# Reordering the start of a two-layer attention and experts kernel, with gate weights, PSUM pools and two operations moved between engines

## The chip, the core and the metric

The kernel runs on one core of a Trainium2 chip. The metric is device time in microseconds (us) of one execution. The core has TensorE (PE, with its weight loads shown apart as PEld), VectorE (DVE), ScalarE (ACT), GpSimd (POOL) and SyncE (SP), which here issues DMAs. Each engine runs its own instructions in order and waits for others on semaphores.

## The reference

The input x is 8 batches of 512 tokens of 256 values, in float32. There are two layers, each a layer norm, two branches, and a residual sum:

```python
xn = _layernorm(x)
x = x + attention(xn) + experts(xn)      # first layer
xn = _layernorm(x)
x = x + reads(xn) + blocks(xn)           # second layer
```

The attention has 16 heads of 64. Queries and keys are RMS-normalised by head. Scores get a bias of distance times a slope by head (`softplus(omega)` times a fixed slope) times a gate by query token, which is `softplus` of the raw-normalised key times a unit vector u by head, over 8:

```python
q = _rmsnorm(q, q_rms_w); k = _rmsnorm(k, k_rms_w)
u_n = u / jnp.maximum(jnp.linalg.norm(u, axis=-1, keepdims=True), U_L2_EPS)
gate = jax.nn.softplus(jnp.einsum('bthd,hd->bht', k, u_n) / math.sqrt(D))
bias = -dist * omega_eff * gate          # causal, then softmax over the scores
```

The experts branch takes 32 experts; each picks 8 tokens of each batch by a softmax over the tokens, merges them, runs a GELU network of 1024 hidden values, and gives the result back to the picked tokens. The second layer is a small GELU read and a block network of 16 blocks, of which each token uses 4.

## The kernel before

**Tiling.** Tokens of a batch are 4 tiles of 128. Heads are in 4 groups of 4, so that there are 32 pieces of work (8 batches by 4 groups), numbered n. `produce(n)` (L584) makes queries, keys, values and gate logits of a group: for each of 4 tiles, `pq` (queries and keys, one 128x512 PSUM tile, L597), `pv` (values and gate logits, L605), a square on ACT (L612), a sum by head on DVE (L629), mean (L632), an inverse root on POOL (L205), the scaled copy `tm` on DVE (L639), its transposes `pqk` (L655), and the copies qT on ACT and kT on DVE (L660, L667). `gate` (L693) then makes the gate's series on DVE (L305 to L312), splits it into bfloat16 parts on POOL (L730 to L751), and turns it (L768, L775: gT). `attend(u)` (L789) does one of 8 units of a group: scores (L807 with the bias rows `bst` and gT, L811 with qT and kT), the maximum (L820), exp (L828), reciprocal (L835), the division on POOL (L838), the transposes `pp` (L851), copies (L859, L861), and after four units the values `y` (L885). `output` (L903) projects (L915).

**Before the first group.** `norm_rows` (L383) loads a batch, takes statistics (L408, L410, L412), an inverse root on POOL (L414), normalises on DVE (L417), transposes (L425) and copies (L434, L436). The first batch goes tile by tile, the other seven whole. `gate_weights` (L340) folds u into the key weights: for a group, squares and sums of u (L347, L351), the root on POOL (L358), floor and reciprocal (L354, L361), u times that and times the key norm's weights (L362, L364), then two products with the key weights and two sums (L368, L370). Their results are the last 4 columns of `wvg_sb`, which `pv` reads. POOL makes the constants of the scores: `masks` (L236) and `bias_rows` (L244 to L261), and the zeros of `mT` (L264). `choose(half)` (L482) picks tokens for the experts once 4 batches are normalised (`lg` L493, `pst` L516, `pmg` L528, `pmT` L541); `expert` (L974) follows.

**What sets the order.** Every piece is an `op` of a class `Plan` (L49): an engine, a cost in ns, a function that issues the instructions, what it depends on, a priority in attention units, and slots that it takes and gives back (`acq`, `rel`: PSUM and SBUF buffers). `emit` (L67) walks a model of the five engines. At each step it takes the operation that can start first, the one of lowest priority where two are equal, of those within 12 units (`AHEAD`) of the lowest priority still open, and issues it. So the costs and priorities fix the order in which each engine's queue is written; at run time only semaphores and those queues count. Three PSUM pools have two buffers each: `mm`, `sc`, `tr` (L173 to L175). SP is the only issuer of DMAs (`load`, L266, whose cost is 60 unless given; weights have 655).

The priorities that matter: u at -19, weights of the first group at -18, gate weights at -17 for the first group and at -1, 1, 3 for the others, `masks` and `bias_rows` at -8 and -7 with no dependency, batches 1 to 3 at 2, 4, 6, the first choice at 8, batches 4 to 7 at 10 to 16, the second choice at 18.5, experts from unit 32 on in steps of 6.5.

Of the kernel before, what the change touches and what calls it, by code (L numbers as in the profile page):

```python
# [15 lines left out]
P = 128  # L16
# [123 lines left out]
def tile_two_layer_block(  # L140
# [82 lines left out]
    with tc.tile_pool(name="pb", bufs=2) as pb, tc.tile_pool(name="pb1", bufs=1) as pb1:  # L223
# [20 lines left out]
        def bias_rows():  # L244
            nc.gpsimd.iota(bst, pattern=[[0, NPR], [1, T]], base=-MID, channel_multiplier=0,
                           allow_small_or_imprecise_dtypes=True)

            for h in range(2):
                k = slice(h * D, (h + 1) * D)
                for q in range(NPR):  # L250
                    r0 = 2 * NSP * q
                    for first, fill in ((r0 + NSP, 1.0), (r0 + 2 * NSP, 0.0)):
                        nc.gpsimd.affine_select(
                            out=bst[k, q, :], in_=bst[k, q, :], compare_op=ALU.is_ge, fill=fill,
                            base=first - 1, pattern=[[0, T]], channel_multiplier=-1,
                        )
                    if q:
                        nc.gpsimd.affine_select(
                            out=bst[k, q, :], in_=bst[k, q, :], compare_op=ALU.is_ge, fill=0.0,
                            base=-r0, pattern=[[0, T]], channel_multiplier=1,  # L260
                        )  # L261

        consts = [op("POOL", 2000, masks, (), -8.0), op("POOL", 5500, bias_rows, (), -7.0)]
        zeros = op("POOL", 2000, lambda: nc.gpsimd.memset(mT, 0.0), (), 4.0)  # L264

        def load(dst, src, prio, cost=60, acq=()):  # L266
            return op("DMA", cost, lambda: nc.sync.dma_start(dst, src), (), prio, acq=acq, lat=2000)
# [3 lines left out]
        for g in range(NHG):  # L271
            at = -18.0 if g == 0 else -9.0 + g
            w_qk[g], w_v[g] = [], []
            heads = slice(g * GW, (g + 1) * GW)
            for dc in range(NC):
                rows = slice(dc * P, (dc + 1) * P)
                w_qk[g].append(load(wqk_sb[:, dc, g, GW:], wk[rows, heads], at, 655))
            for dc in range(NC):
                rows = slice(dc * P, (dc + 1) * P)
                w_qk[g].append(load(wqk_sb[:, dc, g, :GW], wq[rows, heads], at + 0.1, 655))  # L280
                w_v[g].append(load(wvg_sb[:, dc, g, :GW], wv[rows, heads], at + 0.2, 655))
# [4 lines left out]
            load(w128[h * D : (h + 1) * D, k : k + 1], r.unsqueeze(1), -15.5)  # L286
# [34 lines left out]
        for k, f in enumerate(log1p_steps(lambda: oz, lambda: oy, lambda: oy2, lambda: om_sb)):  # L321
# [12 lines left out]
        v_u = [  # L334
            load(ub, u.rearrange("h d -> (h d)").partition_broadcast(P), -19.0, 600, acq=["eh"]),
            load(kwb, k_rms_w.partition_broadcast(P), -18.9, acq=["gT"]),
        ]
        w_g = {}

        def gate_weights(g, at):  # L340
            m = Grp()
            mine = ub3[:, g * HG : (g + 1) * HG, :]
            wide = lambda k: wqk_sb[:, k, g, GW:].rearrange("p (h d) -> p h d", d=D)

            def squares():
                m.sq = pb.tile([P, 2 * HG, D], F32, tag="sq", name=f"usq_{g}", bufs=1)
                nc.vector.tensor_mul(m.sq[:, :HG], mine, mine)  # L347

            def norms():
                m.un = pb.tile([P, HG], F32, tag="un", name=f"un_{g}")  # L350
                nc.vector.tensor_reduce(m.un, m.sq[:, :HG], AX.X, ALU.add)  # L351

            def floor():
                nc.vector.tensor_scalar(m.un, m.un, U_EPS, None, ALU.max)  # L354

            d = [op("DVE", 334, squares, v_u, at, acq=["sq"])]
            d = [op("DVE", 334, norms, d, at + 0.01)]
# [18 lines left out]
        for g in range(NHG):  # L376
            gate_weights(g, -17.0 if g == 0 else -3.0 + 2 * g)
# [1233 lines left out]
```

## Time and profile before

| what | us |
|---|---|
| median of 3 runs | 1491.2 (1490.54 to 1491.31) |
| the profiled execution's own time | 1489.48 |
| its span, first to last instruction | 1487.8 |
| PE busy | 1430.8 |
| DVE, ACT, POOL busy | 906.4, 715.0, 600.4 |
| first transpose of tokens on PE (L425) | 16.39 after the span's start |
| first scores (L807) | 63.45 |

The span is the time from the first to the last instruction of one execution; about 1.7 us lie outside it. A row of the timeline has the start, the length, the engine, the line of the program, the operation, what it writes and reads, the count of merged instructions, and in brackets how long the engine was idle before it and what it waited for. A row of busy time by windows has, after the stretch and its length, the busy us and the count of instructions for PE, PEld, DVE, ACT and POOL, then the granted clock of PE (1.00 is full), the busy share of the DMA engines, and GB/s.

### The profile page before, as it was taken

Reading aid. Unit: us, or ns where it says so; the run is one execution under the profiler, and the core shown is the slowest. Engines: PE = TensorE matmul, PEld = TensorE weight load, DVE = VectorE, ACT = ScalarE, POOL = GpSimd, SP = SyncE. Lnnn points to the kernel's source line nnn. Section 1 sums busy time; section 2 is a strip of 40 time slices with the busy share of each in tenths; the row PEclk is TensorE's granted clock in tenths of the full one; section 3 lists DMA queues with packets and bytes.
Section 4 is the critical chain, followed back from the end, with each engine's and each line's share of the span. In section 5 each row is a group of like instructions: output and inputs, shape, how many; then the busy total and the mean of one; then the engine's idle time right before and its main releaser. Section 6 shows DMA issues by size and latency. Waiting matters only on the chain.

```text
span 1487.8 us, 25107 instructions
## 1 busy us (share of the span) xinstructions
PE 1430.8 (96%) x8317; PEld 866.3 (58%) x8332; DVE 906.4 (61%) x3461; ACT 715.0 (48%) x1928; POOL 600.4 (40%) x1109
## 2 busy tenths in 40 slices
PE   3999999999999999999999999999999899999999
PEld 1555556556655665566556655665566466566666
DVE  6888776676677667766776677667766632322210
ACT  1455555555555556555655565655554531222221
POOL 5544554454454345444454454445444421111100
PEclk9999999999999999999999999999999999999999
DMA  6010111232231321232132213122220000000000
GB/s 203 4 57 1 61 61 60 73 111 65 81 102 59 103 85 57 63 105 80 58 118 65 65 62 114 65 69 85 79 74 9 1 15 15 11 18 15 19 15 22
DMA packets 74688, 90.19 MB, mean 61 GB/s; under 512 B 5800, under 2 KB 57760, under 8 KB 74560
## 3 DMA queue, kind: packets, MB, share of 16 engines
q1 hardware_dynamic: 74560, 88.59, 18.4%
q8 instruction: 67, 1.10, 0.3%
q14 instruction: 61, 0.50, 0.1%
HBM read 84.11 MB, written 4.19 MB: 59 GB/s over the span
## 4 chain that ended last, share of the span: by engine, by line
PE 86%; DVE 8%; ACT 3%; issue 1%; POOL 1%; DMA 1%; SPq 0%; ACTq 0%; DVEq 0%; POOLq 0%
PE pq L597 14%; PE pp L851 9%; PE y L885 8%; PE sc L811 8%; PE ph L1497 8%; PE py L1544 7%; PE po L915 7%; PE pv L605 7%; PE pqk L655 4%; PE sc L807 4%; PE peo L1052 2%; PE ph L992 2%; DVE pr L820 1%; ACT pr L828 1%; DVE ss L629 1%
## 5 line engine op out<-in xcount | busy, mean ns | idle before, releaser
L838 POOL TENSOR_SCALAR pr<-pr,rinv 128x384 f32<-128x384 f32 (+3 forms) x512 | 266.2, 533 | 324.9 <-DVE rinv L835 243.2
L828 ACT ACTIVATE pr<-pr,nm 128x384 f32<-128x384 f32 (+3 forms) x512 | 284.2, 557 | 112.6 <-DVE nm L820 72.8
L205 POOL TENSOR_TENSOR rsqk<-ss,nhalf 128x8 f32<-128x8 f32 x128 | 210.6, 1646 | 218.2 <-DVE ss L632 199.0
L820 DVE CUSTOM_DVE_ANT_0 pr<-sc,later 128x384 f32<-128x384 f32 (+3 forms) x512 | 238.8, 483 | 39.1 <-PE sc L811 35.7
L597 PE MATMUL pq<-wqk_sb,xnT 128*128 128x512 f32 x512 | 248.4, 608 | 2.6 <-DVE gl L623 2.6
L851 PE MATMUL pp<-ident,pr 128*128 128x128 f32 x1280 | 220.0, 282 | 10.6 <-POOL pr L838 2.8
L851 PEld LDWEIGHTS pp<-ident,pr 128*128 128x128 f32 x1280 | 149.7, 141 | 128.6 <-issue 67.8
L811 PE MATMUL sc<-kT,qT 64*128 64x384 f32 (+3 forms) x1024 | 181.9, 437 | 0.0
L859 ACT COPY prT<-pp 128x384 f32<-128x384 f32 (+3 forms) x256 | 107.6, 423 | 147.3 <-PE pp L851 146.4
L861 DVE COPY prT<-pp 128x384 f32<-128x384 f32 (+3 forms) x256 | 124.2, 486 | 72.1 <-PE pp L851 68.4
L885 PE MATMUL y<-prT,v 128*64 128x512 f32 (+3 forms) x1024 | 152.9, 439 | 2.2 <-ACT prT L859 1.8
L605 PE MATMUL pv<-wvg_sb,xnT 128*128 128x260 f32 x512 | 138.3, 393 | 2.3 <-DVE tm L639 2.3
L597 PEld LDWEIGHTS pq<-wqk_sb,xnT 128*128 128x128 f32 x512 | 88.5, 193 | 78.2 <-issue 67.1
L612 ACT ACTIVATE sq<-pq 128x512 f32<-128x512 f32 x128 | 76.2, 595 | 113.9 <-PE pq L597 98.9
L885 PEld LDWEIGHTS y<-prT,v 128*64 128x64 f32 x1024 | 69.1, 136 | 96.4 <-issue 65.3
L1497 PE MATMUL ph<-xT,mT 128*128 128x512 f32 x256 | 121.1, 595 | 0.6 <-DVE nm L820 0.2
L915 PE MATMUL po<-wp_sb,yT 128*128 128x256 f32 x512 | 116.1, 380 | 0.1
L629 DVE TENSOR_REDUCE ss<-sq 128x8 f32<-128x512 f32 x128 | 87.0, 680 | 37.8 <-ACT sq L612 37.5
L605 PEld LDWEIGHTS pv<-wvg_sb,xnT 128*128 128x128 f32 x512 | 89.6, 192 | 32.3 <-issue 9.4
L639 DVE TENSOR_TENSOR tm<-pq,rsqk 128x512 f32<-128x512 f32 x128 | 87.8, 686 | 31.7 <-POOL rsqk L205 30.8
L915 PEld LDWEIGHTS po<-wp_sb,yT 128*128 128x128 f32 x512 | 95.1, 190 | 13.0 <-issue 0.3
L1552 DVE TENSOR_TENSOR ot<-py,x 128x256 f32<-128x256 f32 x32 | 13.6, 424 | 143.7 <-PE py L1544 143.7
(259 smaller groups left out, 1885.4 us busy)
## 6 DMA issues: line engine op xcount, KB each, us to landing
ew<-in_L_ffn_w_dram SPq DMA_DIRECT2D x128, 512.0 KB
xr<-in_L_attn_x_dram SPq DMA_DIRECT2D x32, 128.0 KB
out_dram<-ot SPq DMA_DIRECT2D x32, 128.0 KB
x<-in_L_attn_x_dram SPq DMA_DIRECT2D x7, 512.0 KB
raw<-in_L_ffn_w_dram SPq DMA_DIRECT2D x4, 512.0 KB
wqk_sb<-in_L_attn_Wk_dram SPq DMA_DIRECT2D x8, 128.0 KB
wqk_sb<-in_L_attn_Wq_dram SPq DMA_DIRECT2D x8, 128.0 KB
wvg_sb<-in_L_attn_Wv_dram SPq DMA_DIRECT2D x8, 128.0 KB
```

What stands on the lines that cost most here:

```text
L205: nc.gpsimd.tensor_tensor(r, src, nhalf[:, :n], ALU.pow)
L597: nc.tensor.matmul(s.pq[t], xnT[b][:, dc, cols], wqk_sb[:, dc, g, :], start=(dc == 0), stop=(dc == NC - 1),)
L605: nc.tensor.matmul(s.pv[t][:, : GW + HG], xnT[b][:, dc, cols], wvg_sb[:, dc, g, :], start=(dc == 0), stop=(dc == NC - 1),)
L811: nc.tensor.matmul(m.sc[:, h, :w], s.qT[k, q, n0:w], s.kT[k, q, :w], start=False, stop=True)
L820: nc.vector.tensor_tensor_reduce(m.p[:, h, :], m.sc[:, h, :w], later[:, T - w :], -1.0, BIG, ALU.add, ALU.min, m.nm[:, h : h + 1],)
L828: nc.scalar.activation(m.p[:, h, :], m.p[:, h, :], AF.Exp, bias=m.nm[:, h : h + 1], scale=-1.0, accum_out=m.sums[:, h : h + 1],)
L838: nc.gpsimd.tensor_scalar(m.p[:, h, :], m.p[:, h, :], m.rinv[:, h : h + 1], 1.0, ALU.mult, ALU.mult)
L851: nc.tensor.transpose(m.pt[h][:, d * P : (d + 1) * P], m.p[:, h, j * P : (j + 1) * P], ident)
L861: nc.vector.tensor_copy(dst, src)
L885: nc.tensor.matmul(pp.yp[h * D : (h + 1) * D, j * P :], s.v[j][:, hh * D : (hh + 1) * D], pp.tri[:, h, j : j + 4 * (NT - 1 - j) + 1 : 4, : ...
L915: nc.tensor.matmul(o.po[:, :C], yT[b * nk + k][:, t * P : (t + 1) * P], wp_sb[:, k, :], start=(k == 0), stop=(k == nk - 1),)
L1497: nc.tensor.matmul(m.ph[:, i, :], w1T[:, dc, k * P : (k + 1) * P], s.xT[:, dc, :], start=(dc == 0), stop=False,)
```

## The change

It has these parts.

1. **Order.** `masks` and the new `row_scales` depend, in the plan, on the roots of the first gate weights and of the first batch (`first`). A new op `begun` issues nothing; it depends on the first group's queries, keys and gate rows, and the gate weights of the other groups, the statistics of batches 1 to 7 and the transposes of the experts' gate wait for it in the plan. Batches 1 to 3 go to 5, 10, 15, the first choice to 19, batches 4 to 7 to 21, 25, 29, 33, the second choice to 38, and the experts start 16 units later with steps of 6.0.
2. **Loads.** Weights of a group are one DMA each for keys, queries and values, not two; u is loaded by group (128 KB, not 512 KB at once). Those of the first group's u and values, and of the key norm's weights, are issued by ACT. Costs of loads in the plan are 470 to 900.
3. **Gate weights.** The square is on ACT. The key weights are multiplied with u times the norm's weights, for both halves at once, while the root is taken, and the sums are multiplied with the reciprocal at the end.
4. **Score rows.** `bst` is made of a ramp `pos` by two ACT instructions (scale and bias by partition), with small selects on POOL; before, an iota and ten selects on POOL of 512 columns.
5. **Norms.** For batches 1 to 7 the normalised tokens are written by ACT, with a small DVE step ahead (`nb`).
6. **PSUM.** In the first group, `pq` of tiles 0 and 1 is in `sc` and every `pv` in `tr`. In every group a `pq` follows, in the plan, the `pv` before the last.
7. The zeros of `mT` are eight memsets, not one.

```diff
-        consts = [op("POOL", 2000, masks, (), -8.0), op("POOL", 5500, bias_rows, (), -7.0)]
-        zeros = op("POOL", 2000, lambda: nc.gpsimd.memset(mT, 0.0), (), 4.0)
+        pos = pb.tile([P, T], F32, tag="pr1", name="pos", bufs=1)
+        rows = pb1.tile([P, 2, NPR], F32, tag="rows", name="rows")
+        def row_scales():
+            nc.gpsimd.iota(pos, pattern=[[1, T]], base=-MID, channel_multiplier=0,
+                           allow_small_or_imprecise_dtypes=True)
+            nc.gpsimd.memset(rows, 1.0)
+            for h in range(2):
+                k = slice(h * D, (h + 1) * D)
+                for j in range(2):
+                    first = NSP * j
+                    nc.gpsimd.affine_select(
+                        out=rows[k, j, :], in_=rows[k, j, :], compare_op=ALU.is_ge, fill=0.0,
+                        base=-first, pattern=[[-2 * NSP, NPR]], channel_multiplier=1,
+                    )
...
+        def bias_rows(q):
+            nc.scalar.activation(
+                bst[:, q, :], pos, AF.Identity, bias=rows[:, 1, q : q + 1],
+                scale=rows[:, 0, q : q + 1],
+            )
...
+            w_qk[g] = [
+                load(wqk_sb[:, :, g, GW:], both(wk), at, 900),
+                load(wqk_sb[:, :, g, :GW], both(wq), at + 0.1, 900),
+            ]
+            w_v[g] = [load(wvg_sb[:, :, g, :GW], both(wv), at + 0.2, 900, by=by)]
...
+        begun = op("POOL", 1, lambda: None, (), -6.9)
...
+            d = [op("ACT", 272, squares, v_u[g] + ([begun] if g else []), at, acq=["sq"])]
+            s = [op("DVE", 334, lambda: nc.vector.tensor_reduce(
+                m.un, m.sq[:, :HG], AX.X, ALU.add), d, at + 0.01)]
             d = [op("DVE", 334, lambda: nc.vector.tensor_mul(
-                mine, mine, m.un.unsqueeze(2).to_broadcast([P, HG, D])), d, at + 0.05)]
+                mine, mine, kwb.unsqueeze(1).to_broadcast([P, HG, D])), d, at + 0.015)]
+            r = [op("POOL", 1030, lambda: nc.gpsimd.tensor_tensor(m.un, m.un, phalf, ALU.pow),
+                    s, at + 0.02)]
...
+            d = [op("DVE", 598, products, d + s + w_qk[g][:1], at + 0.07)]
+            d = [op("DVE", 598, lambda: nc.vector.tensor_reduce(
+                m.gw.rearrange("p k h -> p (k h)"), m.sq, AX.X, ALU.add), d, at + 0.08)]
+            w_g[g] = [op("DVE", 86, lambda: nc.vector.tensor_mul(
+                wvg_sb[:, :, g, GW:], m.gw, m.un.unsqueeze(1).to_broadcast([P, NC, HG])),
+                d + r, at + 0.09, rel=["sq"] + (["eh", "gT"] if g == NHG - 1 else []))]
...
-            gate_weights(g, -17.0 if g == 0 else -3.0 + 2 * g)
+            gate_weights(g, -15.95 if g == 0 else -3.0 + 2 * g)
...
+                    if b:
+                        xn = op("ACT", 370, lambda t=t: nc.scalar.activation(
+                            m.x[:, t, :], m.x[:, t, :], AF.Identity, bias=m.ve[:, t : t + 1],
+                            scale=m.rs[:, t : t + 1]), [nb], a_ + 0.1)
...
+        first = roots[:1] + roots[-NT:]
+        consts = [op("POOL", 1000, masks, first, -8.0)]
+        sc_ = op("POOL", 2000, row_scales, first, -7.9, acq=["pr1"])
+        for q in range(NPR):
+            consts.append(op("ACT", 485, lambda q=q: bias_rows(q), [sc_], -7.0,
+                             rel=["pr1"] if q == NPR - 1 else []))
         for b in range(1, BPG):
-            norm_rows(b, 2.0 * b, [list(range(NT))])
-        choose(0, 8.0)
+            norm_rows(b, 5.0 * b, [list(range(NT))])
+        choose(0, 19.0)
         for b in range(BPG, B):
-            norm_rows(b, 10.0 + 2.0 * (b - BPG), [list(range(NT))])
-        choose(1, 18.5)
+            norm_rows(b, 21.0 + 4.0 * (b - BPG), [list(range(NT))])
+        choose(1, 38.0)
...
+                qk_in = "sc" if n == 0 and t < 2 else "mm"
+                v_in = "mm" if n else "tr"
...
-                a = op("PE", 1716, q_k, x_T[b] + w_qk[g], at + w, acq=["mm"])
+                a = op("PE", 1716, q_k, x_T[b] + w_qk[g] + vals[-2:-1], at + w,
+                       acq=[qk_in])
...
         for n in range(NIT):
             produce(n)
+            if n == 0:
+                begun.deps += grp[0].ready
...
-        step = (NIT - NHG - 2) * NU / (4 * NG)
+        step = (NIT - NHG - 4) * NU / (4 * NG)
```

## The prediction

> **What bounds the kernel now.** The page comes first: the share of each engine, the forty slices, and the granted clock.
>
> ```profile
> PE 1430.8 (96%) x8317; PEld 866.3 (58%) x8332; DVE 906.4 (61%) x3461; ACT 715.0 (48%) x1928; POOL 600.4 (40%) x1109
> ...
> PE   3999999999999999999999999999999899999999
> ...
> PEclk9999999999999999999999999999999999999999
> ```
>
> TensorE (PE) is busy 96% of the span, and the only slice below 8 tenths is the first. So the time is PE's work, plus PE's idle time, plus what it does at a lower clock. The diff adds no matmul; only the last two can move. Second, busy time by windows (columns: stretch, its length, then busy us and count for PE, weight loads, DVE, ACT and POOL, then granted clock, DMA share, GB/s):
>
> ```profile
> 0.00:10.00 10.00, 0.00 (x0) 0.00 (x0) 3.45 (x14) 1.28 (x1) 8.83 (x40) 1.00 0.69 187
> 10.00:20.00 10.00, 2.27 (x9) 1.52 (x10) 6.03 (x21) 0.59 (x2) 6.04 (x8) 1.00 0.63 184
> 20.00:30.00 10.00, 7.39 (x15) 3.19 (x14) 7.86 (x35) 0.74 (x2) 2.02 (x2) 1.00 0.76 236
> 30.00:40.00 10.00, 5.69 (x17) 3.69 (x18) 8.84 (x32) 2.34 (x6) 5.44 (x4) 0.59 0.47 150
> 40.00:50.00 10.00, 7.46 (x26) 3.89 (x26) 9.11 (x31) 3.01 (x7) 3.81 (x3) 0.90 0.05 13
> 50.00:60.00 10.00, 9.30 (x41) 5.86 (x40) 8.72 (x42) 4.47 (x11) 5.36 (x11) 1.00 0.01 2
> ```
>
> PE is busy 32.1 of the first 60 us, and part of that at a clock of 0.59 and 0.90. Half of PE's 57 idle us of the whole span (1487.8 less 1430.8) lie here. Third, the timeline says why:
>
> ```profile
> 2.95 0.43 DVE L408 BATCH_NORM_STATS2 ast<-x 128x6 f32<-128x256 f32 x1 [2.95 <-DMA x<-in_L_attn_x_dram]
> ...
> 7.99 2.61 POOL L253 TENSOR_SCALAR_AFFINE_SELECT bst<-bst 64x512 bf16<-64x512 bf16 x4
> 8.16 0.72 DVE L347 TENSOR_TENSOR usq<-ub 128x256 f32<-128x256 f32 x1 [2.89 <-DMA ub<-in_L_attn_u_dram]
> ...
> 11.36 1.02 POOL L358 TENSOR_TENSOR un<-un,phalf 128x4 f32<-128x4 f32 x1
> ...
> 12.36 2.08 POOL L414 TENSOR_TENSOR ars<-ave,nhalf 128x1 f32<-128x1 f32 x4
> ...
> 16.39 1.34 PE L425 MATMUL pxT<-ident,x 128*128 128x128 f32 x4 [16.39 <-DVE x L417]
> ...
> 32.13 0.69 PE L425 MATMUL pxT<-ident,x 128*128 128x128 f32 x2 [4.08 <-DVE x L417]
> ...
> 63.45 0.34 PE L807 MATMUL sc<-gT,bst 64*128 64x384 bf16 x2 [0.16 <-DVE gT L775]
> ```
>
> The tokens are there at 2.95, but their root (L414) stands on POOL behind the score constants, which end at 11.27, and behind the root of the gate weights, which needs the 512 KB of u that land at 8.16. DVE then waits for omega (landed at 13.6, L318) ahead of L417. PE begins at 16.39, stops 4.08 us at 28.05 while DVE works on gate weights and the second batch, and the first score comes at 63.45.
>
> **The sum to compare: time to the first score, less PE's work done by then.** At full clock the rows give 0.30 a tile for pxT (x4 in 0.60), 1.9 for pq, 1.0 for pv, 0.55 for pqk. By 63.45 PE has done 16 x 0.30 + 7 x 1.9 + 7 x 1.0 + 6 x 0.55 + 0.5 (pg, pgt) = 28.9 us: the first group, most of the second, and the transposes of four batches. **Head loss before: 63.45 - 28.9 = 34.5 us.**
>
> **The head after, step by step.**
> - Loads. SP issues x0, x1, the keys' and queries' weights as one DMA each, x2, x3 at about 0.45 us (row: x4 in 1.81), so six until 3.5 instead of twelve until 6.4; the other groups' weights and u are 12 issues for 18, before they are used. ACT takes u of the first group, kwb and the values' weights; the trace has no DMA issue on ACT, so I bound it: 0.43 us each as on SP, before or after ACT's table load (0.78 to 2.06), so u is issued at 0.8 to 2.1 and, 128 KB now, lands at 3 to 5. Four small loads of 0.6 us and omega then end on SP near 6.6, and omega lands near 9.5 (it took 2.9), off the chain. Up to the queries' weights 256 + 160 + 512 = 928 KB move; before, x and u, 1024 KB, were in at 8.16. I take 7.3.
> - First tokens. 2.95, stats, aggregate and eps to 3.97, POOL 0.52 at once (it is free at 3), L417 0.34, two slow transposes 0.69, a copy 0.42: 6.2, before the weights. First pq from 7.3, 3.41 as the slow one before (19.95 on): 10.7.
> - Gate weights. Square on ACT (0.37, the nearest row L434), reduce 0.42, root 1.02, u x kwb 0.41, one product and one reduce of 512 elements (0.69 and 0.68 as L639 and L629), three small ones 0.5: about 9, before pv is due. DVE's part is 2.7 a group against 3.6, so 3.6 us less in all, which lies beside PE's work.
> - The other tiles. PE went to full speed 5.0 us after its matmuls became dense (19.95 to 25: pv took 1.81, the next pq 1.98). So pq1 until 13.6, then pv0, pq2, pv1, pq3 = 5.8: 19.5. The PSUM pools let pq0 and pq1 sit in sc and pv in tr, where before pq t2 (39.73) came 13.9 us after pq t1 (25.83), with two mm buffers held by the roots.
> - Last tile: sq 0.60, ss 0.68, mean 0.16, root 1.65, tm 0.69, gl 0.15, with hand-overs: 23.6.
> - Gate chain. From gl at 51.45 to the first score it took 12.0 before, with work of other batches between. Its rows alone (small DVE ones 3.4, ACT 0.21, POOL 2.24, pgt 0.39, gT 0.41, hand-overs) are 7.4. I take 8.4, since later norms and gate weights are ordered behind the first group: **first score at 32** (28 to 38).
> - Moved constants: masks 0.82 and row_scales on POOL, about 2.2 (an iota under the 0.99 of L245, eight selects of two columns at 0.18 to 0.29, an estimate from L239 and L253), beside the weights' landing; two rows on ACT at 0.68 (L500). If POOL runs them ahead of the first rsqk, 3 us come on the chain; that is in the 38.
>
> PE's work done by 32: 4 pxT 1.2, 6 pq 11.4 (two of the second group need only x and weights), 4 pv 4.0, 6 pqk 3.3, pgt 0.2 = 20.1. **Head loss after: 11.9; gain 22.6** (26.6 to 16.6).
>
> **What is late next.** The second group's gate weights, and so its pv and its third pq, are ordered behind the first score (by `begun`, which issues nothing and adds no semaphore: what waits is only the place in each engine's queue). Up to this pv only scores and transposes of the first group feed PE, and the choice (lg, pst, pmg, pmT: 4.8 us) and later norms no longer fill the first 16 attention units (about 72 us at 4.5 us a unit, 63 to 1220 for 256). Two rows bound it. With fill, 60 to 140 us had 4.6 idle in 80. Without it, before the second layer:
>
> ```profile
> 1140.00:1160.00 20.00, 18.33 (x130) 11.01 (x127) 15.29 (x60) 10.82 (x30) 7.77 (x11) 1.00 0.01 2
> 1160.00:1180.00 20.00, 15.96 (x114) 9.06 (x113) 17.19 (x79) 13.55 (x35) 13.83 (x30) 0.91 0.01 1
> ```
>
> That is 5.7 in 40, or 10 in 72, and a clock of 0.91. So the extra loss is 0 to 6, and up to 8 with dips of the clock. Against it stand 8.8 us of projections that come later than before and fill. I take **5**, nearer to the poor rows.
>
> **Costed at nothing.** 28 normalised tiles go from DVE (0.44 each) to ACT at 0.47 (L660, a scaled copy of the same shape): 13 us on an engine 48% busy and spread over 40 units; without that cover perhaps 2 us, through exp (L828) being late. Eight memsets for one of 1.8 on POOL: the same work in pieces that a divide can pass. Experts start 16 units later with steps of 6.0 for 6.5 units: same end, and 2 MB a step in 27 us is 78 GB/s against the 236 moved above. The plan's order changes everywhere, worth 3 us either way: 400 to 1200 has 13.7 idle us of such kind.
>
> The trace shows that the granted clock fell to half after the 4.08 us stop, for about ten us. The Trainium skill ("TensorE: Matmul & The Clock Gate", on the HAM clock gate) says PE drops to half clock after an idle window of about 3.4 us and returns after a busy one. By that rule the waits of the gate chain (19.5 to 32) could cost one dip, 2 to 4 us, which would move the first score, not the forecast's sign. The skill's "ScalarE: Activation LUTs" (rules for kernel authors) speaks against the moved norms: it gives add and multiply to VectorE, and by its 280 ns + 0.83 a column and 93 ns for a second pointer a tile would be 0.59, 3 us more of ACT in all; the row of L660 is lower.
>
> **Sum.** 22.6 - 5 = 17.6 off. The profiled execution took 1489.48, of which 1487.8 is span; it would become 1471.9. It lies 1.7 under the median, so for the median 1491.2 - 17.6 = **1473.6**.
>
> **Rivals.**
> - Forecast, 0.52: between 1468 and 1479.
> - More, 0.14: first score near 28 and no loss behind it: 26.6 off, 1464.6. For it: DVE, the busiest, has only some 23 us of work there (statistics 3.0, tokens 2.2, gate weights 2.7, four tiles of 2.3, omega 2.5, series 3.4). Against: it would have to run nearly without gaps.
> - Less, 0.17: first score at 36 to 38 and 8 lost behind: 9 to 11 off, 1481. For it: POOL needs 1.65 a root, and the gate chain of 12.0 may stay.
> - Nothing, 0.06: the order written by the plan keeps POOL's constants or the waiting om steps ahead on the chain: within 3 us (0.2%, what a measurement can tell here).
> - Slower, 0.11: the second group is the bound. Its chain starts at the first score with 5 us of gate weights; before, a group took 26 us from its second pv (37.07) to its score. If each of groups two and three starts its scores 13 us after PE ran dry, 26 is lost and 1495 results. It decides from 11.3 us a group. Against it: the first group's 8 units hold 19 us of PE work, and about 10 of projections fill beside it.
>
> Faster 0.52 + 0.14 + 0.17 = 0.83, same 0.06, slower 0.11. The range goes from 1464 to 1487: it leaves out the slower case and the edges.
>
> **What will show it.** First pxT near 5 (16.39), first pq near 7.3, first score near 32; POOL's constants behind L414; no stop of 4 us before pxT; the second group's pv within 6 us of the first score. Wrong if PE's idle time in the 70 us after the first score exceeds 15, or if the first score stays behind 45.

## The result and the profile after

The changed kernel takes 1485.33 us (median of 17 runs, 1483.98 to 1488.2), the kernel before beside it 1490.54 (17 runs): a ratio of 0.9971, with an interval of 0.9963 to 0.9978. So it is faster, by 5.2 us by the medians (4.3 by the ratio) where 17.6 were forecast. Runs of one kernel spread over up to 6 us, the longer ones at a lower granted clock (the kernel before in e1's record: 1486.23 at 0.994, 1491.14 at 0.991), so that some 2 us between two medians is near what can be told here. The profiled execution has a span of 1484.2, against 1487.8.

The page of the changed kernel, its share of PE, the forty slices and the clock:

```profile
PE 1431.3 (96%) x8332; PEld 867.1 (58%) x8332; DVE 894.0 (60%) x3428; ACT 731.3 (49%) x1964; POOL 598.7 (40%) x1115
...
PE   5899999999999999999999999999999899999999
...
PEclk9899999999999999999999999999999999999999
```

PE's work is the same (1430.8 before). The first slice went from 3 to 5 tenths, but the second fell from 9 to 8, at a clock of 8 tenths. Busy time by windows of the changed kernel (same columns as above):

```profile
0.00:10.00 10.00, 0.00 (x0) 0.00 (x0) 3.54 (x15) 1.70 (x2) 4.91 (x31) 1.00 0.48 148
10.00:20.00 10.00, 8.27 (x19) 4.43 (x20) 6.60 (x31) 3.41 (x7) 4.96 (x18) 1.00 0.91 273
20.00:30.00 10.00, 8.83 (x36) 5.46 (x35) 5.36 (x18) 4.15 (x10) 5.66 (x4) 1.00 0.94 300
30.00:40.00 10.00, 5.03 (x19) 2.40 (x17) 7.23 (x27) 2.27 (x5) 5.64 (x14) 0.94 0.12 36
40.00:50.00 10.00, 8.38 (x35) 5.04 (x35) 7.09 (x29) 3.98 (x13) 4.85 (x11) 0.54 0.00 0
50.00:60.00 10.00, 9.49 (x54) 5.58 (x54) 9.79 (x43) 6.28 (x18) 5.51 (x8) 1.00 0.05 16
```

From 10 to 30 PE is busy 17.10 us of 20, where it was 9.66 before. From 30 to 40 it starves (5.03), and from 40 to 50 it works at a clock of 0.54. The start of the timeline tells why PE is not there before 10:

```profile
4.53 0.43 DVE L431 BATCH_NORM_STATS2 ast<-x 128x6 f32<-128x256 f32 x1 [4.53 <-DMA x<-in_L_attn_x_dram]
...
6.19 0.43 DVE L431 BATCH_NORM_STATS2 ast<-x 128x6 f32<-128x256 f32 x1 [1.23 <-DMA x<-in_L_attn_x_dram]
6.53 0.16 DVE L433 BATCH_NORM_AGGREGATE amv<-ast 128x2 f32<-128x6 f32 x1
...
7.15 1.12 POOL L386 TENSOR_TENSOR un<-un,phalf 128x4 f32<-128x4 f32 x1 [4.26 <-DVE ave L435]
...
8.18 0.69 DVE L376 TENSOR_TENSOR usq<-wqk_sb,ub 128x512 f32<-128x512 f32 x1 [0.70 <-DMA wqk_sb<-in_L_attn_Wk_dram]
8.25 1.55 POOL L437 TENSOR_TENSOR ars<-ave,nhalf 128x1 f32<-128x1 f32 x2
...
9.60 0.39 DVE L452 TENSOR_SCALAR x<-x,amv,ars 128x256 f32<-128x256 f32 x1
...
10.04 0.72 PEld L460 LDWEIGHTS pxT<-ident,x 128*128 128x128 f32 x4 [10.04 <-DVE x L452]
```

The first tokens arrive at 4.53 (2.95 before). DVE then waits for the second tile's tokens before it finishes the first tile's statistics, and POOL makes the gate weights' root (7.15) ahead of the token root (8.25). DVE writes the normalised tokens from 9.60 on, and the first weight load on PE waits for them. On PE's part of the timeline:

```profile
10.04 1.12 PE L460 MATMUL pxT<-ident,x 128*128 128x128 f32 x4 [10.04 <-DMA w<-in_L_attn_q_rms_w_dram]
12.81 1.35 PE L460 MATMUL pxT<-ident,x 128*128 128x128 f32 x4 [1.65 <-issue]
13.96 3.62 PE L644 MATMUL pq<-wqk_sb,xnT 128*128 128x512 f32 x4
...
35.30 0.63 PE L702 MATMUL pqk<-ident,tm 128*128 128x128 f32 x4 [1.48 <-DVE gp L328]
39.04 1.09 PE L702 MATMUL pqk<-ident,tm 128*128 128x128 f32 x4 [3.11 <-DVE tm L686]
40.29 0.61 PE L818 MATMUL pgt<-ident,gtm 128*128 128x128 bf16 x4 [0.16 <-POOL gtm L791]
41.54 0.51 PE L857 MATMUL sc<-gT,bst 64*128 64x384 bf16 x2 [0.64 <-DVE gT L825]
...
47.38 1.23 PE L652 MATMUL pv<-wvg_sb,xnT 128*128 128x260 f32 x2
```

The first queries (L644, x4 a tile) stand behind the transposes of all four tiles (12.81). The first score comes at 41.54, 21.9 us earlier than before. Ahead of 35.30 and of 39.04 PE stops for 1.48 and 3.11 us, and the second group's values (47.38) come only after the first scores.

**Where the time went.** For a balance I count as loss the length of a stretch less PE's busy time times its granted clock, added over windows of 10 us. What is left over, PE's work at full clock, is 1419 to 1425 in all profiles, so the balance is good to 3 us either way. Two things widen it. It is that of one profiled run, while the medians are of several. And the clock column reads 1.00 up to its first change, although the first queries take 3.62 us and the next ones (18.76) 1.88: this slow start counts as work here, and differs (in e6 the first queries take 3.02).

| kernel | median | loss | 0 to 60 | 60 to 200 | 200 to 600 | 600 to 800 | 800 to 1000 | 1000 to 1200 | after |
|---|---|---|---|---|---|---|---|---|---|
| before | 1490.5 | 64.0 | 31.0 | 7.1 | 3.3 | 1.3 | 1.8 | 9.0 | 10.5 |
| changed | 1485.3 | 62.3 | 24.2 | 9.1 | 2.3 | 6.0 | 1.5 | 8.7 | 10.6 |
| e1 | 1479.7 | 54.3 | 19.1 | 5.0 | 2.3 | 5.9 | 1.4 | 10.9 | 9.6 |
| e14 | 1480.2 | 57.2 | 21.2 | 7.8 | 2.5 | 4.5 | 1.5 | 8.7 | 11.1 |
| e3 | 1482.1 | 58.2 | 25.1 | 6.4 | 3.3 | 1.3 | 1.8 | 9.0 | 11.2 |
| e16 | 1491.6 | 66.4 | 25.4 | 7.2 | 6.1 | 5.7 | 1.4 | 9.8 | 10.7 |
| e6 | 1481.6 | 59.8 | 23.3 | 7.2 | 2.3 | 5.7 | 1.5 | 8.7 | 11.1 |
| e10 | 1477.5 | 53.1 | 17.7 | 6.1 | 2.2 | 6.2 | 1.6 | 8.5 | 10.7 |
| e13 | 1473.0 | 48.6 | 17.6 | 4.6 | 3.3 | 1.3 | 2.2 | 8.2 | 11.4 |
| e15 | 1477.3 | 54.7 | 17.4 | 9.4 | 3.8 | 1.3 | 1.9 | 9.3 | 11.9 |

The first score came 21.9 us earlier, but by 60 only 6.8 are won; 2.0 are given back by 200, and 4.7 between 600 and 800, in a stretch for which the forecast had no cost. In all the loss falls by 1.7, where the profiled spans differ by 3.6 and the medians by 5.2: what lies between is within the balance's error and the spread of runs.

### The profile page after: what moved, and what is told of

Its sections match the earlier page's. It is cut to its first block, busy times and chain, and to the rows that moved or that the text cites. A ratio compares the mean times of both kernels' runs of the same rounds, so it can differ in the third digit from the quotient of the medians.

```text
span 1484.2 us, 25093 instructions
## 1 busy us (share of the span) xinstructions
PE 1431.3 (96%) x8332; PEld 867.1 (58%) x8332; DVE 894.0 (60%) x3428; ACT 731.3 (49%) x1964; POOL 598.7 (40%) x1115
## 4 chain that ended last, share of the span: by engine, by line
PE 85%; DVE 7%; ACT 4%; issue 1%; POOL 1%; DMA 1%; ACTq 0%; SPq 0%; POOLq 0%; DVEq 0%
PE pq L644 13%; PE pp L901 10%; PE y L935 9%; PE sc L861 8%; PE ph L1549 8%; PE py L1596 8%; PE po L965 7%; PE pv L652 6%; PE pqk L702 3%; PE sc L857 3%; PE ph L1042 2%; PE peo L1102 2%; DVE pr L870 1%; ACT pr L878 1%; PE ph L1553 1%
## 5 line engine op out<-in xcount | busy, mean ns | idle before, releaser
L878 ACT ACTIVATE pr<-pr,nm 128x384 f32<-128x384 f32 (+3 forms) x512 | 284.9, 558 | 99.1 <-DVE nm L870 67.2
L870 DVE CUSTOM_DVE_ANT_0 pr<-sc,later 128x384 f32<-128x384 f32 (+3 forms) x512 | 238.6, 483 | 35.5 <-PE sc L861 27.0
L644 PE MATMUL pq<-wqk_sb,xnT 128*128 128x512 f32 x512 | 248.3, 608 | 0.6 <-DVE gl L670 0.4
L901 PE MATMUL pp<-ident,pr 128*128 128x128 f32 x1280 | 220.5, 282 | 16.8 <-POOL pr L888 4.7
L644 PEld LDWEIGHTS pq<-wqk_sb,xnT 128*128 128x128 f32 x512 | 88.8, 193 | 72.2 <-issue 65.4
```

The lines of the kernel that those rows point to most:

```text
L644: nc.tensor.matmul(s.pq[t], xnT[b][:, dc, cols], wqk_sb[:, dc, g, :], start=(dc == 0), stop=(dc == NC - 1),)
L870: nc.vector.tensor_tensor_reduce(m.p[:, h, :], m.sc[:, h, :w], later[:, T - w :], -1.0, BIG, ALU.add, ALU.min, m.nm[:, h : h + 1],)
L878: nc.scalar.activation(m.p[:, h, :], m.p[:, h, :], AF.Exp, bias=m.nm[:, h : h + 1], scale=-1.0, accum_out=m.sums[:, h : h + 1],)
L901: nc.tensor.transpose(m.pt[h][:, d * P : (d + 1) * P], m.p[:, h, j * P : (j + 1) * P], ident)
```

## The experiments

Each kernel is the changed one with the edit shown; medians are of 4 to 12 runs. Ratios are to the kernel before, run on the same chip. Differences to the changed kernel are between medians from several chips, on which the kernel before had medians of 1489.19 to 1490.54.

**e1: nothing waits for `begun`.**

```diff
-            d = [op("ACT", 272, squares, v_u[g] + ([begun] if g else []), at, acq=["sq"])]
+            d = [op("ACT", 272, squares, v_u[g], at, acq=["sq"])]
-                            [ld] + ([begun] if b else []), a_)
+                            [ld], a_)
-        tg = op("PE", 150, turn_gw, [v_g, begun], 4.0, acq=["tr"], mode="G")
+        tg = op("PE", 150, turn_gw, [v_g], 4.0, acq=["tr"], mode="G")
```

> The changed kernel without the op begun: gate weights of groups two to four, statistics of batches one to seven and the experts' gate may be written ahead of the first scores again. In the changed kernel PE lost 14.8 us (idle, and excess at half clock) between the first score at 41.5 and 200 us, against 6.8 us in the kernel before between 63.5 and 200. Theory Hold (the second group's gate weights come too late, PE starves behind the first score): the second group's first pv, at 47.4, comes before 40, the half-clock stretch of 40 to 50 us goes, the first score comes at most 4 us later, and the time falls by 3 to 6 us. Theory Fill (the choice, the norms and the experts that were put later no longer fill the first two groups): pv comes early too, but the loss up to 200 us stays above 12 us and the time stays within 2 us. Theory Head (all is decided before the first score): the first score comes 4 us later or more and the time rises by as much.

Measured: 1479.69, ratio 0.9932 (0.992 to 0.9944), 5.6 us less than the changed kernel. The second group's first values come at 36.20, as theory Hold has it; the first score comes 5.4 later (46.98), and still the loss up to 60 is 5.1 less. Windows of 3.4 us around the slow stretch, first of the changed kernel:

```profile
35.50:38.90 3.40, 0.43 (x4) 0.19 (x2) 2.24 (x9) 0.47 (x1) 2.30 (x5) 1.00 0.01 2
38.90:42.30 3.40, 2.46 (x12) 1.79 (x14) 1.62 (x5) 0.78 (x2) 2.56 (x13) 0.50 0.00 0
42.30:45.70 3.40, 2.59 (x16) 1.64 (x14) 2.84 (x11) 1.29 (x4) 1.12 (x1) 0.50 0.00 0
45.70:49.10 3.40, 3.40 (x10) 1.57 (x7) 2.43 (x13) 1.31 (x7) 1.65 (x3) 0.50 0.00 0
49.10:52.50 3.40, 3.40 (x16) 2.13 (x15) 2.70 (x12) 1.89 (x5) 1.64 (x3) 1.00 0.02 5
```

then of e1:

```profile
28.90:32.30 3.40, 0.42 (x4) 0.45 (x5) 3.40 (x17) 0.98 (x3) 3.03 (x2) 1.00 0.63 191
32.30:35.70 3.40, 3.40 (x7) 1.23 (x6) 2.97 (x13) 0.69 (x2) 2.15 (x3) 0.52 0.13 39
35.70:39.10 3.40, 2.16 (x11) 1.46 (x10) 2.09 (x12) 1.67 (x4) 0.75 (x2) 0.98 0.00 0
```

In both the clock halves after a window with 0.4 us of PE work. In e1 the second group's work fills the next window (3.40 of 3.40), and the clock is full again after one. In the changed kernel there is only the gate chain and the first scores to run (2.46, 2.59), and the clock stays at half for 10.2 us. So the order after `begun` costs more than it saves.

**e14: only the gate weights are free of `begun`** (the first of e1's three lines).

> The changed kernel where only the gate weights of groups two to four no longer wait for begun in the plan; the statistics of batches one to seven and the experts' gate still do. Theory Gates (the second group's pv is what came too late): nearly all of the 5.6 us, 1479 to 1481.5, the second group's first pv ahead of 42 us, and only a short half-clock stretch or none between 38 and 55 us. Theory Norms (the early statistics and transposes of the second batch fill PE): 1484 to 1486.

Measured: 1480.17, ratio 0.9945 (0.9932 to 0.9958). The second group's first values come at 35.13, not 47.38, and the 10.2 us at half clock become two of 3.4. So most of e1's gain lies in the gate weights alone (5.2 of 5.6 by the medians, some 4 of 6 by the ratios).

**e2: u, the key norm's weights and the values' weights are issued by SP again, behind the tokens.**

```diff
-            w_v[g] = [load(wvg_sb[:, :, g, :GW], both(wv), at + 0.2, 900, by=by)]
+            w_v[g] = [load(wvg_sb[:, :, g, :GW], both(wv), at + (0.45 if g == 0 else 0.2), 900)]
-        v_kw = load(kwb, k_rms_w.partition_broadcast(P), -23.8, acq=["gT"], by="ACT")
+        v_kw = load(kwb, k_rms_w.partition_broadcast(P), -23.55, acq=["gT"])
-                -23.9 if g == 0 else -9.1 + g, 500, acq=["eh"] if g == 0 else [],
-                by="ACT" if g == 0 else "DMA",
+                -23.6 if g == 0 else -9.1 + g, 500, acq=["eh"] if g == 0 else [],
```

> The changed kernel with the three loads that ACT issued (u of the first group, the key norm's weights, the values' weights of the first group) issued by SP instead, behind the first two token tiles and, for the values' weights, behind all four. Theory Landing (the first token tile came at 4.5 us instead of 2.95 since u's load runs beside it, and the fourth tile's load waits for u to land, since eight loads are out at most): the first statistics start at 3.0 to 3.2, the first transposes on PE at 7 to 8.5 instead of 10.0, the first score 1.5 to 3 us before 41.5, and the time falls by 1 to 3 us. Theory Order (the order of the queues on DVE and PE decides, not the landing): statistics start earlier, but the first pq stays at 13.5 to 14.5 and the first score within 1 us.

Measured: 1484.79, ratio 0.9965 (0.9951 to 0.9979). The tokens land early again (2.88) and the first transposes move from 10.04 to 8.4, but the first queries stay at 13.9, behind the last tiles' transposes (12.75), and the first score at 40.8. The landing alone does not decide; the order behind it does, as theory Order has it.

**e6: queries and values of the first batch depend on the tokens of their own tile alone.**

```diff
-                a = op("PE", 1716, q_k, x_T[b] + w_qk[g] + vals[-2:-1], at + w,
+                own = x_T[b] if n else x_T[b][t : t + 1]
+                a = op("PE", 1716, q_k, own + w_qk[g] + vals[-2:-1], at + w,
-                v = op("PE", 876, val, x_T[b] + w_v[g] + w_g[g], at + w + 0.01, acq=[v_in])
+                v = op("PE", 876, val, own + w_v[g] + w_g[g], at + w + 0.01, acq=[v_in])
```

> The changed kernel, where in the first group pq and pv of a tile depend in the plan on the transposed tokens of that tile, and no longer on those of all four tiles. The first pq then stands on PE's queue ahead of the transposes of tiles 2 and 3. Theory Order (the first pq, at 14.0 and not at the 7.3 that I had predicted, waits for nothing but its place behind the transposes of tile 3): the first pq starts at 11.5 to 12.2, the first score 1.5 to 2.5 us before 41.5, and the time falls by 1.5 to 2.5 us. Theory Landing (the queries' weights are not there before 13 us): the first pq stays at 13 to 14 and the time within 1 us.

Measured: 1481.63, ratio 0.9952 (0.9939 to 0.9965), 3.7 us less than the changed kernel. Its timeline on PE:

```profile
10.42 1.12 PE L460 MATMUL pxT<-ident,x 128*128 128x128 f32 x4 [10.42 <-DMA w<-in_L_attn_q_rms_w_dram]
11.63 3.02 PE L644 MATMUL pq<-wqk_sb,xnT 128*128 128x512 f32 x4
...
38.18 0.50 PE L858 MATMUL sc<-gT,bst 64*128 64x384 bf16 x2 [0.65 <-DVE gT L826]
```

The queries follow the first two tiles at once (11.63, not 13.96), and the first score is 3.4 earlier. My forecast had taken for granted that a tile's queries follow its own tokens; but the plan's `x_T[b]` holds all four tiles.

**e9: e6 and e2 together, and the first two tiles' tokens ordered ahead of the gate weights on DVE.** In the plan the sum of u's squares waits for the first two tiles' statistics, and the product with the key weights for their normalised tokens (the lines that fill the two lists are left out):

```diff
+        early_g[0].deps += early_x[0:3:2]
+        early_g[1].deps += early_x[1:4:2]
```

> The changed kernel with the head as I had thought of it when I predicted: pq and pv of a tile follow that tile's tokens alone, SP issues all loads (the first two token tiles, then u), and in the plan the sum of u's squares follows the first tile's statistics and the product with the key weights follows that tile's normalised tokens. Theory Order (what put the first pq at 14.0 instead of 7.3 is order and u's load alone): first transposes at 5 to 6.5, first pq at 7 to 9.5, first score at 35 to 37.5, time 1478 to 1480.5. Theory Landing (the queries' weights are not there before 10.5): the first pq stays at 10.5 to 11.7, as with the own-tile order alone, and the time at 1481 to 1482.

Measured: 1483.38, ratio 0.996 (0.9944 to 0.9975), but the seven runs lie at 1479.85 to 1480.14 (three) and 1483.38 to 1486.05 (four), and the profile is of the longest. In it the first queries come at 9.97, yet the first score at 39.3, later than e6's 38.18:

```profile
7.59 0.43 DVE L384 TENSOR_TENSOR ub<-ub,kwb 128x256 f32<-128x256 f32 x1 [1.33 <-DMA kwb<-in_L_attn_k_rms_w_dram]
...
9.97 6.24 PE L648 MATMUL pq<-wqk_sb,xnT 128*128 128x512 f32 x8 [0.46 <-ACT xnT L471]
```

The queries of the first two tiles take 6.24 us, where they take 3.76 at full clock. The last tile's then start at 22.14, after e6's 21.43, and from them to the score it is 17.2, against 16.8 in e6. So most of the head start is lost ahead of the last queries, to the slow start and a wait of 0.64 us for the last tokens (at 17.96), and 0.4 in the chain to the score. What is left from 7.3 to 9.97 is order again: the token roots end at 5.36, but on DVE the normalised tokens (7.93) stand behind u times the key norm's weights, which land at 7.59.

**e3: batches, choices and experts back at their old places** (priorities and steps of the kernel before).

```diff
-            norm_rows(b, 5.0 * b, [list(range(NT))])
-        choose(0, 19.0)
+            norm_rows(b, 2.0 * b, [list(range(NT))])
+        choose(0, 8.0)
-            norm_rows(b, 21.0 + 4.0 * (b - BPG), [list(range(NT))])
-        choose(1, 38.0)
+            norm_rows(b, 10.0 + 2.0 * (b - BPG), [list(range(NT))])
+        choose(1, 18.5)
-        step = (NIT - NHG - 4) * NU / (4 * NG)
+        step = (NIT - NHG - 2) * NU / (4 * NG)
-            h0, h1, d0, d1 = ((NHG + 2) * NU + step * (4 * g + k) + 0.7 for k in range(4))
+            h0, h1, d0, d1 = (NHG * NU + step * (4 * g + k) + 0.7 for k in range(4))
```

> The changed kernel with the priorities of before for batches one to seven (2 to 16), the two choices (8 and 18.5) and the experts (from unit 32 in steps of 6.5); begun stays. Theory Fill (the later places take PE's fill away from the first groups and cost 5 us or more): PE's loss between the first score and 200 us falls from 14.8 to below 10 us and the time falls by 3 to 6 us. Theory Hold (the wait of the second group's gate weights is the loss): the half-clock stretch of 40 to 50 us stays and the time changes by less than 2 us, or rises by up to 4 us since DVE has more to do there.

Measured: 1482.09, ratio 0.9951 (0.9939 to 0.9964), 3.2 less. The 10.2 us at half clock are still there, and the head is no better. Most of what is won lies between 600 and 800 (1.3 for 6.0), where no normalisation or choice runs any more.

**e16: old places for batches and choices, new ones for the experts** (e3 without its last two pairs of lines).

> The changed kernel with batches one to seven and the two choices at their old places (2 to 16, 8 and 18.5), and the experts at their new ones (16 units later, in steps of 6.0). All of these at their old places took 3.2 us off. Theory Steps (it is the experts' new step that starves PE between 600 and 800 us, idle 4.5 for 1.3): the time stays at 1484 to 1486, and those 4.5 us stay. Theory Fill (it is the norms and choices): 1481.5 to 1483.5, and less idle time up to 200 us.

Measured: 1491.6, ratio 1.0017 (1.0008 to 1.0026), 6 us more than the changed kernel. The loss between 600 and 800 stays (5.7), so it belongs to the experts' places. But the time is worse than either theory said: a further 3.8 us are lost from 200 to 600, of which PE idles 3.1 between 300 and 350 (0.5 in the changed kernel).

The traces show what the experts' places do. In the changed kernel, between 730 and 740:

```profile
728.37 0.63 ACT L1069 ACTIVATE ehT<-ehT 128x512 f32<-128x512 f32 x1
729.02 1.28 ACT L878 ACT_TABLE_LOAD   x1
...
732.40 1.28 ACT L1069 ACT_TABLE_LOAD   x1
733.70 0.63 ACT L1069 ACTIVATE ehT<-ehT 128x512 f32<-128x512 f32 x1
...
734.71 1.28 ACT L878 ACT_TABLE_LOAD   x1
...
737.91 0.35 ACT L665 COPY v<-pv 128x256 f32<-128x256 f32 x1
...
738.53 0.40 PE L901 MATMUL pp<-ident,pr 128*128 128x128 f32 x1 [2.88 <-DVE gl L670]
```

The two halves of an expert group's GELU (L1069) stand on ACT with exps (L878) between them, so that ACT loads its table of functions twice more, 1.28 us each; the values' copy (L665) stands behind, and PE stops for 2.88 us. In the kernels with the old places (before, e3, e13, e15) no exp stands between the two halves of a group, with 8 loads for the GELU and no such stop; with the new places there are 9, and in e16, where it happens to the first group too (PE stops 2.88 us ahead of 309.91), 10. No run undid this alone.

**e4: all batches but the first normalised by DVE again.**

```diff
-                else:
+                elif False:
-                    if b:
+                    if False:
```

> The changed kernel with the normalised tokens of batches one to seven written by DVE as before (28 tiles at 0.44 us), without the small step ahead of them. Theory Engine (ACT's 28 tiles delay exp, and that is what eats the gain): the time falls by 2 to 5 us. Theory nothing (they lie beside PE's work on either engine): within 2 us, and the first score stays at 41.5 within 0.5 us.

Measured: 1480.99, ratio 0.9944 (0.9932 to 0.9957), 4.3 less.

**e8: e4 and e1 together.**

> The changed kernel without begun and with the normalised tokens of batches one to seven on DVE, the two undoings that took 5.6 and 4.3 us off when made alone. Theory two causes (late gate weights of the second group; ACT held up by the tokens): 1475 to 1477. Theory one cause (both only let PE have other work in the 50 us behind the first score): 1479 to 1481, no better than without begun alone.

Measured: 1481.1, ratio 0.9946 (0.9932 to 0.9961): 1.4 more than e1 alone, so nothing more came off.

**e15: e4 on top of e13 (below).**

> The kernel of e13 (own tile, no begun, old places: 1473.0) with the normalised tokens of batches one to seven on DVE instead of ACT. Made alone on the changed kernel this took 4.3 us off; together with no begun it took nothing more off (1481.1 against 1479.7). Theory Engine (ACT's tiles cost 3 to 4 us): 1469 to 1470.5. Theory nothing (what was gained alone were two dips of PE's clock to half, of 3.4 us each, that fell away): 1472 to 1475.

Measured: 1477.32, ratio 0.992 (0.9908 to 0.9933): 4.3 more than e13. So neither theory held. The same edit gives -4.3, +1.4 (not clear of the spread) and +4.3 in three surroundings. In e4 the half-clock windows at 73 and 738 are gone, in e15 one of 6.8 us at 109 is new (loss from 60 to 200: 9.4 for 4.6). The engine of the norms itself has no price that can be told from where such windows fall.

**e5: nothing but a cost in the plan** (a statistic at 340 ns, not 334).

```diff
-                    st = op("DVE", 334, lambda t=t: nc.vector.bn_stats(m.st[:, t, :], m.x[:, t, :]),
+                    st = op("DVE", 340, lambda t=t: nc.vector.bn_stats(m.st[:, t, :], m.x[:, t, :]),
```

> The changed kernel with one cost in the plan, that of the token statistics on DVE, set to 340 ns for 334: no instruction is added, taken away or changed, some change places in the queues. It tells how much a change of order without meaning moves the time. Theory Plan (the order far behind the first groups is a matter of chance, and moves by several us with any edit, so that no part of 3 to 5 us can be read from one kernel): the time differs from the changed kernel's 1485.3 by 2 us or more. Theory Small: by less than 1.5 us, with the first score at 41.5 within 0.5.

Measured: 1485.12, ratio 0.9972 (0.9961 to 0.9983). This one small shift of the plan moves 0.2 us.

**e7: the first groups' queries and values in the pool `mm` alone.**

```diff
-                qk_in = "sc" if n == 0 and t < 2 else "mm"
-                v_in = "mm" if n else "tr"
+                qk_in = "mm"
+                v_in = "mm"
```

> The changed kernel with all pq and pv of the first group in the two mm buffers as before, instead of sc and tr. Theory Pools (the third pq must not wait for the first root): the first score comes 4 to 8 us later than 41.5, and the time rises by 3 to 6 us. Theory nothing (PE has no better work there, and what is late at the head is made up by the second group): the time stays within 1.5 us.

Measured: 1487.28, ratio 0.999 (0.9981 to 1.0), first score at 44.6. The three pools are worth 3.1 us at the first score and 2.0 in all, less than theory Pools said.

**e17: score rows made by POOL as before, behind the roots.** One operation on POOL with the iota and selects of the kernel before takes the place of `row_scales` and ACT's two rows:

```diff
-        sc_ = op("POOL", 2000, row_scales, first, -7.9, acq=["pr1"])
-        for q in range(NPR):
-            consts.append(op("ACT", 485, lambda q=q: bias_rows(q), [sc_], -7.0,
-                             rel=["pr1"] if q == NPR - 1 else []))
+        consts.append(op("POOL", 5500, old_rows, first, -7.0))
```

> The changed kernel with the rows of the scores made by POOL as before (an iota and ten selects of 512 columns, about 7 us), but still behind the first roots; ACT's two instructions and the small selects are gone. Theory Pool (the first root of queries and keys, at 19.7, stands behind them on POOL): the first such root comes at 21 to 24, the first score 1.5 to 4 us later than 41.5, the time 1 to 3 us higher. Theory nothing (PE is dense there with pq and pv and the order makes up for it): the time within 1 us.

Measured: 1485.29, ratio 0.9972 (0.996 to 0.9984), first score at 41.8. Once the rows stand behind the roots, it does not matter who makes them.

**e10: e1 and e6 together.**

> The changed kernel with a tile's pq and pv after its own tokens (3.7 us off when made alone) and without begun (5.6 off alone). Theory Apart (the one is worth its 2.4 us ahead of the first score, the other behind it): both add up, 1475.5 to 1477.5. Theory Same (both only close the same gap, PE's wait and half clock around the first score): 1479 to 1481.

Measured: 1477.47 (1476.49 to 1480.63), ratio 0.9932 (0.9917 to 0.9947), 2.2 less than e1 by the medians, but with the same ratio: a gain over e1 is not shown. In the profiled run, the shortest, no window at half clock is left from the slow start to 200.

**e13: e1, e6 and e3 together.**

> The kernel before this one in the list, with the priorities of before for batches one to seven, the choices and the experts as well. Alone these took 3.2 us off the changed kernel; PE's idle time from 600 to 800 us went from 4.5 to 1.3, that from 400 to 600 from 1.3 to 2.8. Theory Steps (experts in steps of 6.0 units after 16 units more starve PE in the middle of the run): 600 to 800 has 1 to 2 us of idle time again, and the time is 2 to 3.5 us below that of the kernel before it in the list. Theory Fill (the gain of the old places was in the first 200 us, and is used up): the same within 1.5 us.

Measured: 1472.98 (1472.54 to 1474.47), ratio 0.9896 (0.9882 to 0.991): the best of all, 12.3 us below the changed kernel. By the medians 5.6 of these come with e1, 2.2 more with e6 (not clear, see e10), 4.5 more with e3. The stretch from 600 to 800 in the changed kernel:

```profile
600.00:800.00 200.00, 195.53 (x1224) 116.41 (x1220) 133.70 (x509) 112.02 (x309) 92.40 (x175) 0.99 0.25 80
```

and in e13:

```profile
600.00:800.00 200.00, 198.73 (x1233) 118.48 (x1231) 136.02 (x517) 109.24 (x311) 95.15 (x179) 1.00 0.24 80
```

PE idles 4.5 us in the one and 1.3 in the other; 2.88 of the 4.5 are the stop shown at e16. Every kernel here with the new places of the experts, e16 too, has 4.3 to 4.5 there, every one with the old places (before, e3, e13, e15) 1.3.

## Why the prediction was right in direction and wrong in size

- **What bounds the kernel: right.** PE's work did not move, and the balance of losses accounts for the span of every kernel here to about 3 us either way. PE's work by the first score was 20.1, as worked out.
- **"First score at 32 ... gain 22.6": mis-sized, the first failure.** It came at 41.54, 9.5 late. The head loss was 41.54 - 20.1 = 21.4, not 11.9, and the gain 13.1. The 9.5 are three terms. First, queries at 13.96, not 7.3: 6.7. Of these 2.3 are the other tiles' transposes, as e6 shows. The rest, by the rows, is the tokens' landing at 4.53 (the forecast kept 2.95 from before, with u not yet beside it), the second tile's statistics ahead of the first's aggregate, the gate root (7.15) ahead of the token root (8.25), and DVE's 0.70 wait for the key weights; e9, which mends most of this, has its first queries at 9.97. I had put POOL's root "at once (it is free at 3)" and had not followed the queues of DVE and POOL past the gate weights, which have the better place there. Second, the last tile from the end of its queries to its gate logits: 5.2 for 4.1. Third, the gate chain of 10.1 for 8.4, in which the split on POOL (38.13) stands behind a root of the second group (36.53, 1.64 us). The step between, 12.2 us from the first queries to the end of the last, was right (12.1).
- **"What is late next: 5": the right mechanism, too small.** From the first score to 200 the loss is some 7 to 8 us more (about 14 against 7) than from 63.45 to 200 before. The forecast looked for idle time ("wrong if PE's idle time in the 70 us after the first score exceeds 15"); PE idles only 5.5 there (70.0 less 64.53), and at a mean clock of 0.92 some 5 more are lost. e1 and e14 show the cause: `begun` keeps the second group's gate weights, and so its values, off PE while the clock waits for a full window.
- **"Experts ... same end": wrong, costed at nothing.** The loss after 200 is 3 us larger, all of it between 600 and 800. e16 and e3 show that it goes with the experts' places and steps, and the trace shows one GELU split by exps, with two more table loads on ACT and a stop of 2.88 us on PE. I had weighed DMA traffic and the end, not the order on ACT. Gain and losses together, 13.1 less 7 to 8 less 3, leave 2 to 3 us, near the 1.7 of the balance.
- **The clock.** "One dip, 2 to 4 us" became one stretch of 10.2 us, 4.2 us lost by 60. The Trainium skill ("TensorE: Matmul & The Clock Gate", on the HAM clock gate) gives windows of about 3.4 us, and the stretches here are that or multiples of it (3.4, 6.8, 10.2); but it speaks of an idle window, and here 0.43 of 3.4 busy was enough to lose the clock.
- **Norms on ACT: no price shown, but my row was wrong.** I took 0.47 from L660. The row of the changed kernel:

```profile
L448 ACT ACTIVATE x<-x,ave,ars x28: 584/594/610, 61.3 to 177.6; 128x256 f32<-128x256 f32 x28
```

  (shortest, median and longest, in ns). The Trainium skill's "ScalarE: Activation LUTs" (What ACT_TABLE_LOAD costs), from whose 280 ns, 0.83 ns a column and 93 ns for a pointer I worked out 0.59, agrees with this row and was the better source. The 28 tiles cost ACT 16.6, not 13; e4, e8 and e15 show no steady price in time.
- **Rows on ACT, small shifts of the plan:** nothing, as costed (e17; e5 0.2).
- **The rivals.** "Less" (1481) came nearest: 7 to 8 us were lost behind the first score, near its 8, but the score came at 41.54, past its 36 to 38, and the experts' 3 to 5 are not in it. "Slower" did not come: the second group's values were 5.8 us behind the first score. Its cause, the second group held back, is nevertheless what gave most when one edit undid it (e1, 5.6).
- **The signs I had named** were too coarse: first transposes near 5, queries near 7.3 and the first score near 32 failed, but the masks did go behind the token roots (12.72), no stop of 4 us came before the first transposes, values came within 6 us, idle stayed under 15 and the score under 45.

Open remains what the split GELU costs by itself, since no run undid it alone. That half-clock windows come and go with small shifts, and from run to run, is seen; what sets their phase is not.

## What to carry to other kernels

Price an early start by what the bounding engine lost (length less work at full clock), not by when its first long-awaited instruction comes: e13 has a later first score (48.54) than the changed kernel and is 12.3 us faster. Ahead of a chain that must hand over several times between engines, keep independent matmuls in the queue, since a thin stretch can cost twice, as idle time and as clock. And when an order is written by a plan, follow every dependency of the first instruction (here all four tiles, for one tile's queries) and the queues of the small engines, before a forecast counts from a landing time. When work moves to another place, look at what stands beside it on ACT: two functions in turn cost table loads, 1.28 us each here.

## What the runs showed of the hardware

- The clock that fell after a thin stretch did not return with dense-looking work: windows of 3.4 us with 2.46 and 2.59 us busy left it at half, and it rose after one with 3.40. In the kernel before the same was to be seen from 28.4 on: 0.00 busy, then 1.41, 2.88 and 3.40 at half clock, then full.
- A full stop is not needed for it to fall: it fell after windows of 0.43 (35.5), 1.57 (69.6 to 73.0) and 0.53 (735.2 to 738.6) busy us in the changed kernel.
- Busy time alone does not settle it. In windows of 3.41 us laid from one change of the clock, it fell after 2.21 (before, 120.48) and stayed full after 1.43 and 1.53 (e10, 32.78 to 39.60); it rose after 2.86 (e16, 309.36) and stayed at half after 3.03 (e1, 1155.44).
- The first tokens landed at 4.53 with u issued by ACT at 0.78 beside them, at 2.95 when SP alone issued (before and e9; 2.88 in e2, which differs from the changed kernel in three loads alone).
- ACT loaded a table, 1.28 us, each time it went from exp to GELU or back (changed kernel, 727.08 to 734.71: four loads for two GELU halves of 0.63).
